# The first transformer's P V with the values in the array: dividing P on GpSimd, and whole units as pieces of the order

## The chip, the cores and the metric

The kernel runs on one core of a Trainium2 chip. A core has TensorE (PE; PEld is its weight loading), VectorE (DVE), ScalarE (ACT), GpSimd (POOL) and the queues that issue transfers (SP's is the one that matters here). The time is that of one launch in microseconds of the device; a table gives the median of three runs. The profile is of one further execution.

## The reference

x is 4 x 512 tokens of 128 features in f32. Four layers each compute `x = x + s * silu(f)`, where s and f are two sub-networks of the normalised x:

- layer 0: local and latent attention; a feed-forward with weights and inputs rounded to FP4
- layer 1: causal attention of 16 heads; a ternary gated feed-forward
- layer 2: differential attention; **a transformer of 6 layers with 16 heads of 64, local attention with a window of 32** ("the first transformer", names with `l2`)
- layer 3: a linear recurrence; a transformer of 2 layers with 8 heads and a window of 64 ("the second transformer", `l3`)

One transformer layer:

```
q, k, v = shift_tokens(x) @ Wqkv, in heads of 64
q, k = rotary(l2norm(q) * q_scale), rotary(l2norm(k) * k_scale)
sim = 8 * q k^T        # a block of W queries sees its own and the previous block of W keys
o = softmax(sim) @ v
x = x + o @ Wo
h = layernorm(shift_tokens(x)) ; a, g = h @ W1 + b1
x = x + (a * gelu(g)) @ W2 + b2
```

## The kernel before

Features lie on the partitions and tokens in the free dimension throughout: x is a tile of 128 x 2048. Everything is f32 but the masks.

`transformer` makes three generators over all rows (a row is a layer and one of the four batch elements): `queries_keys`, `attention` and `feed_forward`. The first transformer has two groups of eight heads (GP = 2), so 24 rows x 2 = 48 slots. In slot i it merges a part of each: queries and keys of slot i, attention of an earlier slot, feed-forward of an older one. Each generator yields the estimated TensorE time of the piece that it has just written, and `merge` always continues the one that has done the smallest share of its total (10.3, 20.4, and 7.7 or 1.7). So the pieces set the order of the program; the framework then places the instructions of each engine, mostly in that order, ahead of it where an instruction is ready earlier, and each engine works through its own list in order.

The attention of a slot is two units (j = 0 and 1), of four heads each, at 512 queries. Steps of a unit, with the line numbers of the profile (matrix products all show line 122 or 1389, the helper `net.mm` and the scores' own call; transposes show 126):

- `scores` (L1370): two mask matmuls, then 64 small matmuls of 64 x 32 stationary and 64 columns (L1389) on eight tiles of the array, two row halves by four column quarters; then the row maximum (L1399), two subtractions (L1403), the exponential (ACT, L1408), the row sum (L1410) and the reciprocal r (L1412)
- `turn` (L1415): eight 128x128 transposes of P, and the ACT copy into PT (L1424). It is called for the previous unit, in the middle of the scores
- `weigh` (L1427): P V. 64 small matmuls with PT stationary (64 x 32) and the values streaming (64 columns); the result has queries on the partitions, and two DVE multiplications by r put it into On (L1454)
- `turn_back` (L1465): eight transposes of On, and two ACT copies into OT (L1474)
- after the second unit, the output product: four matmuls of 512 columns with Wo, added to x (L1513)
- `values` (L1331): 16 value products of 64 columns of tokens by 256, in two halves, copied to vo (L1352); four transfers on SP (L1356, L1358) make ve, the copy of vo that is shifted by one block. Values are made two units ahead

All PSUM tiles of the transformer come from one pool of four buffers of two banks (`S2`). `queries_keys` writes each projection into such a buffer; ACT squares it (L1293), POOL adds the halves (L1294), DVE multiplies by two tables (L1295, L1297), POOL adds (L1298). `unit_length` sums the squares on TensorE, takes the root on ACT (L1317, L1318), multiplies on DVE (L1321) and moves the result by eight transfers on SP (L1328). `split` is true in the first transformer alone.

## Time and profile before

| what | value |
|---|---|
| time, median of 3 runs | 3968.79 us (3940.47 to 3970.37) |
| the profiled execution's own time | 3955.01 us |
| its span, first to last instruction | 3953.3 us |
| mean granted TensorE clock | 0.942; 0.99 to 1.00 in the first transformer |
| the first transformer lies at | about 1590 to 3410 us |
| POOL, L1298 (128x1024 addition) | 224 of 2362 ns |
| POOL, L595 (128x1024 by a broadcast, layer 1) | 48 of 1893 ns |
| ACT, L1474 (copies to OT, 128x512) | 192 of 592 ns |
| DVE, L1454 (On, 128x512) | 192, 120.5 us busy, mean 668 ns |

Busy times of one engine are added up from its instructions; a matmul's record is longer than the time that it keeps the array, since matmuls overlap. The distance from start to start of neighbouring matmuls is what one costs. An f32 matmul has two records.

### The profile page before, as it was taken

Reading aid. Unit: us, or ns where it says so; the run is one execution under the profiler, and the core shown is the slowest. Engines: PE = TensorE matmul, PEld = TensorE weight load, DVE = VectorE, ACT = ScalarE, POOL = GpSimd, SP = SyncE. Lnnn points to the kernel's source line nnn. Section 1 sums busy time; section 2 is a strip of 40 time slices with the busy share of each in tenths; the row PEclk is TensorE's granted clock in tenths of the full one; section 3 lists DMA queues with packets and bytes.
Section 4 is the critical chain, followed back from the end, with each engine's and each line's share of the span. In section 5 each row is a group of like instructions: output and inputs, shape, how many; then the busy total and the mean of one; then the engine's idle time right before and its main releaser. Section 6 shows DMA issues by size and latency. Waiting matters only on the chain.

```text
span 3953.3 us, 105287 instructions
## 1 busy us (share of the span) xinstructions
PE 3577.5 (90%) x46763; PEld 1880.3 (48%) x46891; DVE 2452.6 (62%) x3429; ACT 1845.0 (47%) x2510; POOL 1157.9 (29%) x994
## 2 busy tenths in 40 slices
PE   7786999899999998889999999999999999778887
PEld 4553455444444443444444554554444445445554
DVE  6674555413353341677777787777777777457774
ACT  3343666523133324454555554555455455535555
POOL 1000444300021112533334343343443343033220
PEclk7677999999699999999999999999999999889998
DMA  1000000001000001434344434334334333413221
GB/s 38 8 26 28 1 1 1 30 0 51 2 1 3 3 1 37 106 86 115 88 96 110 98 91 109 95 91 119 93 83 117 86 80 94 130 37 83 54 56 42
DMA packets 123574, 236.12 MB, mean 60 GB/s; under 512 B 29624, under 2 KB 44128, under 8 KB 117728
## 3 DMA queue, kind: packets, MB, share of 16 engines
q1 hardware_dynamic: 114064, 209.58, 21.7%
q10 hardware_dynamic: 8624, 19.29, 1.5%
q8 instruction: 369, 6.05, 0.6%
q0 software_dynamic: 432, 0.51, 0.1%
q14 instruction: 85, 0.70, 0.1%
HBM read 50.08 MB, written 5.54 MB: 14 GB/s over the span
## 4 chain that ended last, share of the span: by engine, by line
PE 62%; DVE 13%; ACT 12%; issue 6%; DMA 3%; POOL 2%; SPq 1%; DVEq 0%; ACTq 0%; POOLq 0%
PE S L122 39%; PE S L126 5%; PE M L122 5%; PE S L1389 4%; PE o L1094 3%; ACT l_P L581 3%; PE o L614 2%; DVE l_rot L1295 2%; DVE rotp L1297 1%; DMA l_tab<-in_k_rot_l 1%; DVE l_rot L1321 1%; PE S L1008 1%; ACT sqp L1293 1%; ACT l_PT L1424 1%; SPq L1328 1%
## 5 line engine op out<-in xcount | busy, mean ns | idle before, releaser
L1298 POOL TENSOR_TENSOR l_rot<-l_rot,rotp 128x1024 f32<-128x1024 f32 x224 | 528.6, 2362 | 324.7 <-DVE rotp L1297 313.3
L1294 POOL TENSOR_TENSOR sqp<-sqp 128x512 f32<-128x512 f32 x224 | 291.5, 1301 | 956.6 <-ACT sqp L1293 952.0
L122 PE MATMUL S<-hb,l_wqk 128*128 128x512 f32 x896 | 476.8, 622 | 38.1 <-ACT l_PT L1424 10.7
L1293 ACT ACTIVATE sqp<-S 128x1024 f32<-128x1024 f32 x224 | 230.2, 1027 | 305.1 <-PE S L122 304.1
L1321 DVE SCALAR_TENSOR_TENSOR l_rot<-S,l_rot 128x1024 f32<-128x1024 f32 x224 | 264.6, 1219 | 133.8 <-ACT S L1318 110.6
L126 PE MATMUL S<-core,l_P 128*128 128x128 f32 x1856 | 266.9, 288 | 40.1 <-ACT l_P L1408 17.3
L122 PE MATMUL S<-l_KT,l_QT 32*128 32x256 f32 (+7 forms) x1536 | 264.2, 510 | 34.7 <-ACT l_P L1116 14.5
L1295 DVE TENSOR_TENSOR l_rot<-S,l_tab 128x1024 f32<-128x1024 f32 x224 | 271.2, 1211 | 24.6 <-ACT sqp L1293 24.0
L1389 PEld LDWEIGHTS S<-l_qk 64*32 64x32 f32 (+1 forms) x13312 | 178.5, 108 | 217.7 <-issue 211.2
L1116 ACT ACTIVATE l_P<-S 128x1024 f32<-128x1024 f32 x160 | 156.7, 1022 | 252.3 <-PE S L122 251.7
L126 PEld LDWEIGHTS S<-core,l_P 128*128 128x128 f32 x1856 | 213.3, 146 | 128.1 <-issue 39.3
L1297 DVE TENSOR_TENSOR rotp<-S,l_tab 128x1024 f32<-128x1024 f32 x224 | 270.8, 1209 | 1.4 <-POOL l_rot L1298 1.3
L1389 PE MATMUL S<-l_qk 64*32 64x64 f32 (+1 forms) x13312 | 249.5, 230 | 18.8 <-DMA l_qk<-l_rot 1.7
L122 PE MATMUL S<-sqp,l_k 128*128 128x512 f32 x448 | 251.9, 648 | 13.4 <-POOL sqp L1294 6.6
L122 PE MATMUL S<-l_wv,hb 128*64 128x256 f32 (+1 forms) x1600 | 237.2, 400 | 5.5 <-DVE rotp L1297 4.2
L1069 DVE TENSOR_REDUCE l_mx<-S 128x2 f32<-128x768 f32 (+1 forms) x192 | 155.0, 864 | 136.7 <-PE S L1008 136.7
L122 PEld LDWEIGHTS S<-l_ve,l_PT 64*32 64x32 f32 (+1 forms) x6656 | 164.3, 108 | 152.5 <-issue 124.9
L1399 DVE TENSOR_REDUCE mx<-S 128x16 f32<-128x1024 f32 (+1 forms) x128 | 156.3, 1221 | 116.1 <-PE S L1389 112.2
L122 PEld LDWEIGHTS S<-hb,l_wqk 128*128 128x128 f32 x896 | 147.2, 191 | 168.6 <-issue 92.0
L122 PE MATMUL S<-l_OT,l_wo 128*128 128x512 f32 (+1 forms) x512 | 218.9, 543 | 8.3 <-DVE ffu L1551 7.9
L1120 POOL TENSOR_SCALAR_AFFINE_SELECT l_P<-l_P 128x256 f32<-128x256 f32 x256 | 99.4, 406 | 417.0 <-ACT l_P L1116 411.6
L1317 ACT ACTIVATE S<-S,l_tiny 128x1024 f32<-128x1024 f32 x112 | 121.9, 1089 | 198.4 <-PE S L122 180.2
(358 smaller groups left out, 6580.1 us busy)
## 6 DMA issues: line engine op xcount, KB each, us to landing
l_qk<-l_rot SPq DMA_DIRECT2D x896, 128.0 KB
l_ve<-l_vo SPq DMA_DIRECT2D x112, 256.0 KB
l_ve<-l_vo SPq DMA_DIRECT2D x96, 224.0 KB
l_tab<-in_k_rot_l ACTq DMA_DIRECT2D x16, 1024.0 KB
l_wqk<-in_l2Wqkv SPq DMA_DIRECT2D x12, 512.0 KB
l_wv<-in_l2Wqkv SPq DMA_DIRECT2D x12, 256.0 KB
l_wo<-in_l2Wo SPq DMA_DIRECT2D x12, 256.0 KB
l_ve<-l_vo SPq DMA_DIRECT2D x24, 128.0 KB
```

The source lines that it names most:

```text
L122: self.nc.tensor.matmul(out, lhsT, rhs, start=start, stop=stop)
L126: self.nc.tensor.transpose(out, in_, self.ident[:n, :n])
L1069: nc.vector.tensor_reduce(mxv[:, bs, 2 * m + e, 3 - i], s[u][:, :, c : c + n], axis=AX.X, op=ALU.max)
L1116: nc.scalar.activation(P[u], s[u], AF.Exp, scale=scale)
L1293: nc.scalar.activation(sq, p, AF.Square)
L1294: nc.gpsimd.tensor_tensor(sq[:, 0, :], sq[:, 0, :], sq[:, 1, :], ALU.add)
L1295: nc.vector.tensor_tensor(t[:, g], p, tab[:, 0], ALU.mult)
L1297: nc.vector.tensor_tensor(m, p, tab[:, 1], ALU.mult)
L1298: nc.gpsimd.tensor_tensor(t[:, g], t[:, g], m[:, ::-1, :], ALU.add)
L1321: nc.vector.scalar_tensor_tensor(t[:, g], p[:, g, :].unsqueeze(1).to_broadcast([128, 2, S]), 1e12, t[:, g], ALU.min, ALU.mult)
L1389: net.nc.tensor.matmul(sv[W * bl : W * bl + W, e, t, g, :].rearrange("p (s k) -> p s k", s=2), qk[0][r, g, j, W * c : W * c + W], kw, star ...
L1399: nc.vector.tensor_reduce(mx, flat, axis=AX.X, op=ALU.max)
```

## The change

In the first transformer (`split`):

- P is multiplied by r on GpSimd right after the softmax; the multiplication of On on DVE is gone
- `turn` of the previous unit is called after the softmax of the current one, not in the middle of its scores
- `weigh_turned` takes the place of `weigh` and `turn_back`: the values (64 x 64) are stationary on the four quadrants of the array and 32 columns of PT stream. The result has the head dimension on the partitions and is copied to OT directly. Blocks of odd number have the two heads' halves exchanged, so OT has a second index for the block's parity, and Wo is loaded a second time with its halves exchanged; the output product becomes 2 x 4 matmuls of 256 columns
- the values of a unit pair are made one unit ahead: the first half in the unit before, the second half in the first unit, each ahead of P V
- pieces: the scores of a unit and its P V are one piece each, marked `Small`; after a `Small` piece `merge` continues another generator. Query/key products, sums of squares and value products are handed over in pairs or halves. The attention's total is 18.6
- Wo has two buffers for three

The second transformer keeps `weigh` and `turn_back`; its output product yields after every two matmuls instead of each.

```diff
+class Small(float):
+    pass
...
 def merge(run):
     run, totals = [g for g, _ in run], [t for _, t in run]
     done = [0.0] * len(run)
+    i = piece = None
     while run:
-        i = min(range(len(run)), key=lambda k: done[k])
+        others = [k for k in range(len(run)) if k != i] if isinstance(piece, Small) else []
+        i = min(others or range(len(run)), key=lambda k: done[k])
         try:
-            done[i] += next(run[i]) / totals[i]
+            piece = next(run[i])
+            done[i] += piece / totals[i]
         except StopIteration:
+            piece = None
             del run[i], done[i], totals[i]
...
-        self.attention_weight = 20.4 if self.split else 25.0
+        self.attention_weight = 18.6 if self.split else 25.0
...
-                t = self.WT.tile([128, 4, 128], F32, name=pre + "_wo", bufs=3)
-                nc.sync.dma_start(t, a[pre + "Wo"][l][512 * gp : 512 * (gp + 1)].rearrange("(t p) n -> p t n", p=128))
+                t = self.WT.tile([128, 2 if self.split else 1, 4, 128], F32, name=pre + "_wo", bufs=2)
+                wo = a[pre + "Wo"][l][512 * gp : 512 * (gp + 1)].rearrange("(t p) n -> p t n", p=128)
+                nc.sync.dma_start(t[:, 0], wo)
+                if self.split:
+                    nc.sync.dma_start(t[0:64, 1], wo[64:128])
+                    nc.sync.dma_start(t[64:128, 1], wo[0:64])
...
                             c = 128 * (4 * g + 2 * i + h)
                             o = p[:, h, :]
                             net.mm(o.rearrange("p (s u k) -> p s u k", s=2, k=W) if i else o, w[:, c : c + 128], hk if i else hb)
-                            yield 0.86
+                            if h or not self.split:
+                                yield 1.72 if self.split else 0.86
...
         for g in range(2):
             net.mm(p[:, g, :], self.ones, sums[g][:, 0, :])
-            yield 0.86
+            if g or not self.split:
+                yield 1.72 if self.split else 0.86
...
                 if self.split:
                     for e in range(2):
                         net.mm(pv[64 * e : 64 * e + 64, k - u0, :], hb[:, 64 * k : 64 * k + 64], w[:, 256 * e : 256 * e + 256])
-                    yield 0.45
                 else:
                     c = 128 * (n * tp + k)
                     net.mm(pv[:, k - u0, :], hb[:, c : c + 128], w)
                     yield 0.86
+            if self.split:
+                yield 1.8
...
         for t in range(T):
-            if last and t == T // 2:
+            if last and t == T // 2 and not self.split:
                 yield from self.turn(last)
...
-                yield 0.31
+                if not self.split:
+                    yield 0.31
+        if self.split:
+            yield Small(2.48)
...
         nc.vector.tensor_reduce(rs, P.rearrange("p t g e k -> p (t g e) k"), axis=AX.X, op=ALU.add)
         r = net.stat(n, "r")
         nc.vector.reciprocal(r, rs)
+        if self.split:
+            Pn = P.rearrange("p t g e k -> p (t g e) k")
+            nc.gpsimd.tensor_tensor(Pn, Pn, r.unsqueeze(2).to_broadcast([128, n, 2 * W]), ALU.mult)
+            if last:
+                yield from self.turn(last)
         return P, r
...
+    def weigh_turned(self, u, OT):
+        net, W, T = self.net, self.W, self.T
+        PT, vo, ve, tp, j = (u[k] for k in ("PT", "vo", "ve", "tp", "j"))
+        o = self.S2()
+        ov = o.rearrange("p s (i x q) -> p s i x q", x=2, q=W)
+        for i in range(2 * T):
+            for bl in range(self.NB):
+                c = self.NB * (T * tp + i // 2) + bl
+                v, k = (vo if c % 2 else ve), c // 2 - tp * self.NU
+                for e in range(2):
+                    rows, d, s = slice(64 * e, 64 * e + 64), 64 * (2 * (i % 2) + j), bl % 2
+                    x = 64 * (e ^ s)
+                    net.mm(ov[x : x + 64, s, i, bl // 2, :], v[rows, k, d : d + 64], PT[rows, i, W * bl : W * bl + W])
+        yield Small(2.4)
+        for s in range(2):
+            dst = OT[:, s].rearrange("p (g j) (t q) -> p j g t q", j=2, q=2 * W)
+            self.nc.scalar.copy(dst[:, j], o[:, s, :].rearrange("p (t g q) -> p g t q", g=2, q=2 * W))
...
     def weigh(self, u):
         net, nc, W, T = self.net, self.nc, self.W, self.T
         PT, r, vo, ve, tp, j = (u[k] for k in ("PT", "r", "vo", "ve", "tp", "j"))
         On = self.PP.tile([128, 2 * T, 2, 64], F32, name=self.pre + "_On", bufs=1)
-        o = self.S2() if self.split else self.M()
+        o = self.M()
...
-                    if self.split:
-                        rows, d = slice(64 * e, 64 * e + 64), 64 * (2 * g + j)
-                        net.mm(
-                            o[W * bl : W * bl + W, e, 64 * i : 64 * i + 64], PT[rows, i, W * bl : W * bl + W],
...
-            nc.vector.tensor_tensor(
-                On.rearrange("p n e d -> p (n e) d"), o.rearrange("p (n d) -> p n d", d=64),
-                r.unsqueeze(2).to_broadcast([128, 4 * T, 64]), ALU.mult,
-            )
+                    n, d = 2 * i + e, 64 * (4 * g + 2 * j + e)
+                    net.mm(o[W * bl : W * bl + W, 64 * n : 64 * n + 64], PT[:, n, W * bl : W * bl + W], v[:, k, d : d + 64])
+            yield 0.15
+        nc.vector.tensor_tensor(
+            On.rearrange("p n e d -> p (n e) d"), o.rearrange("p (n d) -> p n d", d=64),
+            r.unsqueeze(2).to_broadcast([128, 4 * T, 64]), ALU.mult,
+        )
         u["On"] = On
...
     def turn_back(self, u, OT):
         net, T = self.net, self.T
-        t = (self.S2() if self.split else self.M().unsqueeze(1)).rearrange("p a (b q) -> p (a b) q", q=128)
+        t = self.M().rearrange("p (b q) -> p b q", q=128)
...
             if older:
-                if older["j"] == 0:
-                    OT = self.TP.tile([128, 4, 128 * T], F32, name=self.pre + "_OT", bufs=1)
-                self.turn_back(older, OT)
-                yield 0.9 if self.split else 0.45
+                if not self.split:
+                    if older["j"] == 0:
+                        OT = self.TP.tile([128, 1, 4, 128 * T], F32, name=self.pre + "_OT", bufs=1)
+                    self.turn_back(older, OT[:, 0])
+                    yield 0.45
                 if older["j"] == 1:
                     wo = self.part("o", older["l"], older["gp"])
                     p = self.M()[:, 0 : 128 * T]
-                    for t in range(4):
-                        net.mm(p, wo[:, t, :], OT[:, t, :], t == 0, t == 3)
-                        yield 0.86 if self.split else 0.43
+                    parities = 2 if self.split else 1
+                    pv = p.rearrange("p (x s q) -> p s x q", s=parities, q=W)
+                    for s in range(parities):
+                        for t in range(4):
+                            net.mm(pv[:, s], wo[:, s, t, :], OT[:, s, t, :].rearrange("p (x q) -> p x q", q=W), t == 0, t == 3)
+                            if t % 2:
+                                yield 0.86
                     ys = net.tok(self.y, older["b"])[:, 128 * T * older["tp"] : 128 * T * (older["tp"] + 1)]
                     nc.vector.tensor_tensor(ys, ys, p, ALU.add)
                 older.clear()
-            if last:
+            if last and not self.split:
                 yield from self.weigh(last)
-            if u and i + 2 < len(units) and u["j"] == 0:
+            if u and self.split:
+                if u["j"] == 0 and i:
+                    yield from until_none(ahead)
+                elif u["j"] == 1 and i + 1 < len(units):
+                    ahead = self.values(units[i + 1])
+                    yield from until_none(ahead)
+            elif u and i + 2 < len(units) and u["j"] == 0:
                 ahead = self.values(units[i + 2])
                 yield from until_none(ahead)
             elif u and i + 1 < len(units):
                 yield from until_none(ahead)
+            if last and self.split:
+                if last["j"] == 0:
+                    OT = self.TP.tile([128, 2, 4, 256], F32, name=self.pre + "_OT", bufs=1)
+                yield from self.weigh_turned(last, OT)
```

## The prediction, made before the change was run

> **What bounds the kernel now.** I read the page's busy rows, then stretches of the first transformer, then its waits, and then TensorE's timeline inside one slot, because a share of busy time does not say what a matmul costs.
>
> ```profile
> PE 3577.5 (90%) x46763; PEld 1880.3 (48%) x46891; DVE 2452.6 (62%) x3429; ACT 1845.0 (47%) x2510; POOL 1157.9 (29%) x994
> ```
>
> Busy time in a stretch of the first transformer, columns PE, weight loads, DVE, ACT, POOL, granted clock:
>
> ```profile
> 2400.00:2600.00 200.00, 191.88 (x3341) 99.11 (x3351) 156.26 (x176) 101.50 (x117) 77.24 (x46) 0.99 0.43 106
> ```
>
> TensorE works 96% of this stretch at full clock, the others 78, 51 and 39%. Between 1800 and 3200 us there are 74 units (the 74 row maxima of L1399), two to a slot: a slot lasts 1400/37 = 37.8 us, and there are 48. TensorE waits about 1.5 us per slot; its longest waits there are short and scattered:
>
> ```profile
> PE S L122 <- DVE l_On L1454: 16.1, 14, 1.4
> PE S L122 <- ACT l_PT L1424: 10.1, 25, 0.8
> ```
>
> So the set of instructions on TensorE decides, and what lies between them. The timeline (start, length, tile, shape, records; an f32 matmul is two records):
>
> ```profile
> 2412.38 0.41 PE L1389 MATMUL S<-l_qk 64*32 64x64 f32 x18
> 2412.72 1.12 PE L122 MATMUL S<-hb,l_k 128*128 128x512 f32 x2
> 2413.77 0.71 PE L1389 MATMUL S<-l_qk 64*32 64x64 f32 x46
> 2414.41 1.09 PE L126 MATMUL S<-core,l_P 128*128 128x128 f32 x8
> 2415.34 1.02 PE L122 MATMUL S<-hb,l_wqk 128*128 128x512 f32 x2
> 2416.29 0.86 PE L1389 MATMUL S<-l_qk 64*32 64x64 f32 x64
> 2417.08 1.09 PE L126 MATMUL S<-core,l_On 128*128 128x128 f32 x8
> 2418.01 1.02 PE L122 MATMUL S<-ffg,core 128*128 128x512 f32 x2
> ...
> 2421.16 1.02 PE L122 MATMUL S<-hb,l_wqk 128*128 128x512 f32 x2
> 2422.02 1.88 PE L122 MATMUL S<-l_OT,l_wo 128*128 128x512 f32 x4
> ```
>
> Starts tell the price. A full matmul among its like takes 2422.02-2421.16 = 0.86 us. Ahead of small tiles it takes 2416.29-2415.34 = 0.95, between two groups of them 2413.77-2412.72 = 1.05. The groups of 18 and 46 take 0.34 and 0.64 us: 0.30 for 28 records, so 10.7 ns each, and 0.34-18x0.0107 = 0.15 us for leaving the small tiles. **One visit to small tiles costs 0.15+0.09+0.10 = 0.34 us** beyond its records. Counting the changes of tile shape along the timeline from 1800 to 3200 us gives 484 visits from the full array, 13.1 a slot, or 4.4 us of 37.8.
>
> **The change part by part**, per slot of two units.
>
> *Turning back goes.* P V now leaves the head dimension on the partitions, so the 16 transposes of l_On fall: 2418.01-2417.08 = 0.93 us per unit, **-1.86**. Its copies stay (two of 128x512 per unit, 592 ns on ACT, the same size). The division of the output goes from DVE: 4 x 0.63 us, off the path; its buffer waits (16.1 us in 37 slots, 0.4 a slot) become waits for the ACT copies that now free it.
>
> *Whole units as pieces.* I followed the pieces through merge with their new weights. A slot's order is: a query/key pair, all scores, feed-forward, turn, a pair, eight output matmuls, a pair, values and P V at once, a pair of sums, all scores, a pair, feed-forward, turn, values and P V at once, a pair of sums. That is four visits: 9.1 fewer, at most -3.1. The trace's order departs here and there from the program's (a feed-forward pair ahead of its place), so I count eight visits: 8 x 0.34 = **-2.7**. If pieces are torn apart again: 0.
>
> *P V with V loaded.* As many records, 128 a unit, but 64 columns are loaded and 32 stream, on four quadrants instead of eight tiles. Now, and in the nearest rows where loading is longer than streaming (32 loaded, 18 streamed):
>
> ```profile
> 2406.84 0.25 PE L122 MATMUL S<-l_ve,l_PT 64*32 64x64 f32 x2
> ...
> 2407.64 0.23 PE L122 MATMUL S<-l_vo,l_PT 64*32 64x64 f32 x2
> 2407.81 0.65 PE L122 MATMUL S<-l_wv,hb 128*64 128x256 f32 x4
> ```
>
> ```profile
> 88.46 0.20 PE L122 MATMUL M<-l_ve,l_PT 128*32 128x18 f32 x1
> ...
> 88.74 0.20 PE L122 MATMUL M<-l_vo,l_PT 128*32 128x18 f32 x1
> ```
>
> The first are 80 records in 0.97-0.15 us: 10.3 ns. The second are 34 in 0.28 us: 8.5 ns, on four column tiles of one row group. Mean load times (128 columns 190 ns, 64 columns 137) give 0.83 ns a column, 27 ns for 32: a tile there comes round in 34 ns, its load and 7 more. The Trainium skill (TensorE: Matmul & The Clock Gate, Part 3, the mechanism) says that a load overlaps running matmuls only in another row group. By that, two quadrants of a row group take turns: (53+27)/2 = 40 ns a record, 5.1 us a unit, +7.5 a slot, and the change loses. But by that rule the second row would need 27+15 = 42 ns a record, and it shows 8.5. I take the row: (53+8)/4 = 15.3 ns, 1.96 us a unit against 1.35, **+1.2**. Bounds: 13.3 (loads alone) +0.7; 30 (two loads at a time) +4.9.
>
> A second rule speaks against it: the Trainium skill (TensorEngine Tiling (Array Packing), Restrictions and Gotchas, Gotcha 1) says that row tiles cannot use one PSUM bank at once, and each bank here takes both row halves, on different partitions. The second transformer's recurrence already writes four row groups into one bank:
>
> ```profile
> 3451.83 7.25 PE L741 MATMUL T<-l_x,l_LW 32*32 32x64 f32 x256 [7.30 <-DVE l_x L855]
> ```
>
> That is 28 ns a record with the clock at 0.73; one at a time would need over 64x0.83 = 53. So they run together.
>
> *Output matmuls* become 16 records of 256 columns in place of eight of 512 per slot: the same columns. The second transformer has that form, 8 records in 3601.81-3599.99 = 1.82 us less the 0.09 of leaving: 0.216 each, half of 0.43. Zero. *Weights of them*: three transfers for one, twelve times, and two buffers for three; SP now waits there 42.0 us in six waits, unseen by TensorE. A buffer still comes free a slot before it is needed; behind it on SP are query/key transfers for a later slot. Zero to 2 us each; I take zero.
>
> *P divided on GpSimd.* Nearest row: L595, the same form (128x1024 times a broadcast), 1893 ns. POOL goes from 14.6 to 18.4 us of a slot. TensorE never waits for POOL in 1800-3200 us. Its cover is a unit's length, some 17 us, before the turn. But POOL works in order: behind a division that waits for the softmax (maximum 1.22, two subtractions 1.3, exponential 1.06, sum 1.22, reciprocal 0.24) stand the additions of squares, for which the sums on TensorE wait.
>
> *Turn moved* behind the next unit's softmax, with its ACT copy (1.02). In a slot's second half only 16 value records (1.7 us) lie between the turn and its P V. If the copy stands behind that unit's exponential, counting from the end of the scores: DVE 2.4 (unit lengths), 1.2, 1.3; ACT 1.06, then the copy, 7.0; TensorE is there at 1.8+0.93+1.7 = 4.4. That wait is 2.6 us where no feed-forward piece lies between, nothing if the copy goes first. *Values* are made a unit before use instead of two to three: their four transfers (issue 0.56 and 0.70 us) stand between two sets of query/key transfers on SP and have about 15 us; landings in the chain took 2.1 us (query/key) to 6.4 (a table of 1 MB). Zero.
>
> For all new waits I put **+0.8**, less the 0.4 of the old buffer waits: +0.4. Bounds -0.4 and +5.
>
> Sum: -1.86-2.7+1.2+0.4 = **-2.96 us a slot, x48 = -142 us**.
>
> **The rivals.**
> - *POOL and ACT stand in line (slower).* The division holds the additions of squares: reciprocal at 7.4 after the scores, division 9.3, addition 10.6, while TensorE asks for the second sum at 4.4+1.96+0.86 = 7.2: 3.4 us once a slot. The late rotation behind it holds a PSUM buffer of four, and the next pair waits about its own 1.7. Then 5.1+0.3 stands for my 0.4: +2 a slot, +96, **about 4060**. It decides above 3.4 us of new waits a slot. For it: in-order queues, DVE at 78%. Against: the DVE rows show rotations slipped in ahead of a row sum that waits, so the order follows readiness.
> - *Half of it goes into waits:* -1.5 a slot, **about 3895**.
> - *It does not do what it says:* order torn up, or loads two at a time. Without the visits: -0.26 a slot, **about 3950**; with loads at 30 ns: +0.7, near 4000.
>
> **How the numbers follow.** The profiled execution took 3955.01 us, span 3953.3. Less 142: 3813. The median of the three runs is 14 above it; I say **3825**, between the two bases. Forecast 0.57 (own range 3770 to 3880), half 0.14, no effect 0.10, slower 0.19. The measurement of this kernel tells about 1% from no change (40 us). Faster 0.71, same 0.10, slower 0.19. Range: low end 9.1 visits, P V at 13.3 and no new waits, -4.3+0.2, some 3770; high end 3960, above which the slower cases lie.
>
> **What would show it.** No l_On rows; P V as 64*64 tiles with 32 columns at 14 to 17 ns from start to start; scores in groups of 128; about 35 us between every second row maximum; DVE near 27 us a slot, POOL near 18. Wrong if P V needs over 29 ns a record, if visits stay above ten, or if TensorE's waits for POOL's squares or ACT's l_PT pass 3 us a slot. The rest, outside 1590 to 3410 us, should not move.

## The result, and the profile after

The changed kernel took **4005.24 us** (median of 4, 3996.53 to 4013.39) against 3966.34 us before on the same chip: 1.0104 times as long, 95% interval 1.0078 to 1.013. It is slower by 39 us; the forecast was 3825.

Engine totals of the changed kernel:

```profile
PE 3483.6 (87%) x46379; PEld 1964.7 (49%) x46507; DVE 2353.1 (59%) x3237; ACT 1903.3 (48%) x2554; POOL 1338.5 (34%) x1090
```

TensorE is busy 94 us less and the kernel is slower all the same, so TensorE waits more. Two stretches of the first transformer (columns as before: PE, weight loads, DVE, ACT, POOL, granted clock):

```profile
2400.00:2600.00 200.00, 171.16 (x3123) 103.51 (x3134) 142.40 (x148) 102.03 (x115) 94.86 (x56) 0.96 0.41 103
2600.00:2800.00 200.00, 164.68 (x3028) 98.74 (x3032) 134.81 (x142) 104.15 (x116) 90.57 (x56) 0.96 0.39 99
```

Where 191.88 of 200 us were busy, 165 to 171 are. TensorE's waits from 1800 to 3200 us (us in total, times, longest) say for what:

```profile
PE S L122 <- DMA l_wqk<-in_l2Wqkv: 80.7, 5, 17.2
PE S L1405 <- issue: 24.2, 29, 1.8
PE S L122 <- ACT l_PT L1448: 20.6, 19, 1.2
...
PE S L122 <- DVE l_rot L1336: 8.3, 9, 0.9
```

The first was not there before at all: five waits of up to 17 us, one at each step to the next layer, for that layer's query/key weights. Slots, taken from every second row maximum, last 35.8 us on average between these steps. The five slots at the steps last 55.6, 56.0, 55.6, 56.3 and 52.5: **97 us beyond the others**.

What SP did before at the first of these steps, and what it does now (start, length, records):

```profile
1807.95 5.14 SPq L1328 DMA_DIRECT2D l_qk<-l_rot  x8
1813.19 0.53 SPq L1229 DMA_DIRECT2D l_wqk<-in_l2Wqkv  x1
```

```profile
1843.45 2.31 SPq L1374 DMA_DIRECT2D l_ve<-l_vo  x2
1852.40 5.13 SPq L1343 DMA_DIRECT2D l_qk<-l_rot  x8
1857.58 1.08 SPq L1237 DMA_DIRECT2D l_wqk<-in_l2Wqkv  x2
```

Before, the load for the first head group went out a slot ahead, at 1813, and the one for the second group at 1854. Now both stand together behind eight query/key transfers, and these start only at 1852.40. DVE and then TensorE of the changed kernel at the same place:

```profile
1845.30 1.23 DVE L1336 SCALAR_TENSOR_TENSOR l_rot<-S,l_rot 128x1024 f32<-128x1024 f32 x1 [0.22 <-issue]
1848.38 1.22 DVE L1336 SCALAR_TENSOR_TENSOR l_rot<-S,l_rot 128x1024 f32<-128x1024 f32 x1 [1.86 <-POOL l_rot L1312]
1852.43 1.42 DVE L1261 TENSOR_SCALAR l_tab<-l_tab,l_cols 128x1024 f32<-128x1024 f32 x2 [2.83 <-DMA l_tab<-in_k_rot_l]
```

```profile
1841.06 1.98 PE L122 MATMUL S<-sqp,l_k 128*128 128x512 f32 x4
...
1861.70 2.05 PE L122 MATMUL S<-hb,l_wqk 128*128 128x512 f32 x2 [16.66 <-DMA l_wqk<-in_l2Wqkv]
```

The load is issued at 1857.58 and TensorE goes on at 1861.70, 4.1 us later: the load is not slow, its place in SP's list is late. What the eight transfers wait for last is not the rotated tile. DVE ends that at 1849.60, and they go when the new layer's table (l_tab) has landed, at 1852.34. So it is at four of the five steps; only at the fifth is DVE the last. SP's own waits, 1580 to 3450 us, list the table with nine waits in all:

```profile
SPq L1343 <- DMA l_tab<-in_k_rot_l: 65.1, 9, 10.2
```

The wait has a second price. The granted clock at this step (columns: PE busy, granted clock, DMA share, GB/s):

```profile
1845.00:1850.00 5.00, 0.04 (x4) 0.88 0.95 303
1855.00:1860.00 5.00, 0.00 (x0) 0.50 0.88 208
1860.00:1865.00 5.00, 3.30 (x4) 0.50 0.55 217
```

The clock falls to half while TensorE stands, and stays there until 1865.9, 4.2 us after it goes on: the two records at 1861.70 take 2.05 us, where two such took 1.02 before. At each of the five steps the trace has such a stretch of 14 to 20 us, which ends 3 to 6 us after TensorE goes on. By estimate (half of the time in which TensorE was busy at half clock) this costs 13 us from 1800 to 3200 us, a part of what the 97 us hold beyond the 80.7 of waiting.

The rest of TensorE's timeline is as forecast. P V and scores of one unit (rows left out between):

```profile
1951.66 1.95 PE L122 MATMUL S<-l_wv,hb 128*64 128x256 f32 x16
1953.54 0.25 PE L122 MATMUL S<-l_PT,l_ve 64*64 64x32 f32 x2
...
1955.54 1.99 PE L122 MATMUL S<-sqp,l_k 128*128 128x512 f32 x4
```

```profile
1935.76 0.69 PE L1405 MATMUL S<-l_qk 64*32 64x64 f32 x45
1937.38 1.06 PE L1405 MATMUL S<-l_qk 64*32 64x64 f32 x83 [0.93 <-issue]
```

128 P V records take 1955.54-1953.54 less 0.15 for leaving, 1.85 us, 14.5 ns each (median over all units 14.6). Scores come 128 in a go, but 0.93 us passes inside this group with nothing to wait for that the profile shows. More of that below.

By stages of the two profiled executions (span 3994.8 against 3953.3, +41.5): the stretch ahead of the first transformer +10.8; the first transformer from its first query/key matmul to its last +9.5; from there to the first one of the second transformer +13.9; the second transformer's own query/key stretch +9.3; the remainder -2.0. The first of these is chance: all these kernels have the same code there, and in the executions profiled below it ends anywhere between 1577 and 1599 us.

### The profile page after: what moved, and what is told of

It reads as the page before. It is cut to its first block, busy times and chain, and to the rows that moved or that the text cites. A ratio compares the mean times of both kernels' runs of the same rounds, so it can differ in the third digit from the quotient of the medians.

```text
span 3994.8 us, 104662 instructions
## 1 busy us (share of the span) xinstructions
PE 3483.6 (87%) x46379; PEld 1964.7 (49%) x46507; DVE 2353.1 (59%) x3237; ACT 1903.3 (48%) x2554; POOL 1338.5 (34%) x1090
## 3 DMA queue, kind: packets, MB, share of 16 engines
q8 instruction: 367, 6.01, 0.6%
## 4 chain that ended last, share of the span: by engine, by line
PE 62%; DVE 12%; ACT 11%; issue 7%; DMA 3%; POOL 3%; SPq 1%; DVEq 0%; ACTq 0%; POOLq 0%
PE S L122 42%; PE M L122 5%; PE S L126 4%; PE o L1102 3%; ACT l_P L581 3%; PE S L1405 3%; DVE l_rot L1336 2%; PE o L614 2%; POOL l_rot L1312 1%; PE S L1016 1%; DVE mx L1418 1%; DVE l_rot L1309 1%; DVE rotp L1311 1%; ACT S L1332 1%; ACT l_P L1124 1%
## 5 line engine op out<-in xcount | busy, mean ns | idle before, releaser
L122 PE MATMUL S<-hb,l_wqk 128*128 128x512 f32 x896 | 459.6, 630 | 119.5 <-DMA l_wqk<-in_l2Wqkv 80.7
L1308 POOL TENSOR_TENSOR sqp<-sqp 128x512 f32<-128x512 f32 x224 | 286.3, 1278 | 664.4 <-ACT sqp L1307 664.2
L1309 DVE TENSOR_TENSOR l_rot<-S,l_tab 128x1024 f32<-128x1024 f32 x224 | 272.7, 1217 | 112.3 <-ACT sqp L1307 111.0
L122 PE MATMUL S<-l_KT,l_QT 32*128 32x256 f32 (+7 forms) x1536 | 274.0, 530 | 33.8 <-ACT l_P L1124 14.5
L122 PEld LDWEIGHTS S<-hb,l_wqk 128*128 128x128 f32 x896 | 159.5, 195 | 259.5 <-issue 199.6
L1311 DVE TENSOR_TENSOR rotp<-S,l_tab 128x1024 f32<-128x1024 f32 x224 | 270.0, 1205 | 1.3 <-POOL l_rot L1312 1.3
L1405 PE MATMUL S<-l_qk 64*32 64x64 f32 (+1 forms) x13312 | 206.5, 231 | 52.0 <-issue 33.7
L122 PE MATMUL S<-l_wv,hb 128*64 128x256 f32 (+1 forms) x1600 | 219.5, 397 | 27.7 <-ACT l_PT L1448 26.1
L122 PE MATMUL S<-sqp,l_k 128*128 128x512 f32 x448 | 227.9, 626 | 12.3 <-POOL sqp L1308 6.0
L122 PE MATMUL S<-l_OT,l_wo 128*128 128x256 f32 x896 | 211.0, 385 | 20.2 <-DVE ffu L1595 17.9
L1405 PEld LDWEIGHTS S<-l_qk 64*32 64x32 f32 (+1 forms) x13312 | 164.9, 108 | 120.4 <-issue 115.8
L122 PEld LDWEIGHTS S<-l_PT,l_ve 64*64 64x64 f32 x6144 | 191.8, 137 | 60.3 <-issue 26.8
L122 PEld LDWEIGHTS S<-l_OT,l_wo 128*128 128x128 f32 x896 | 168.2, 191 | 77.5 <-DVE ffu L1595 36.0
L1434 POOL TENSOR_TENSOR l_P<-l_P,r 128x1024 f32<-128x1024 f32 x96 | 186.3, 1940 | 57.8 <-DVE r L1431 55.6
```

What stands on the lines that cost most here:

```text
L122: self.nc.tensor.matmul(out, lhsT, rhs, start=start, stop=stop)
L1308: nc.gpsimd.tensor_tensor(sq[:, 0, :], sq[:, 0, :], sq[:, 1, :], ALU.add)
L1309: nc.vector.tensor_tensor(t[:, g], p, tab[:, 0], ALU.mult)
L1311: nc.vector.tensor_tensor(m, p, tab[:, 1], ALU.mult)
L1405: net.nc.tensor.matmul(sv[W * bl : W * bl + W, e, t, g, :].rearrange("p (s k) -> p s k", s=2), qk[0][r, g, j, W * c : W * c + W], kw, star ...
L1434: nc.gpsimd.tensor_tensor(Pn, Pn, r.unsqueeze(2).to_broadcast([128, n, 2 * W]), ALU.mult)
```

## The experiments

**What is counted.** Besides times I use two numbers per slot, from some sixteen slots near 2200 to 2800 us. A slot is the time from one unit's row maximum to that of the unit two further on. *Stalled* is the time that TensorE loses: for each pair of neighbouring matmul records, what lies more than 150 ns above the tenth-lowest distance of pairs of this kind (inside groups of small tiles, above their mean). *Own work* is the rest. Before: 37.8 us, of it 1.9 stalled and 35.9 own work. After, the steps between layers counted in: 38.3, 5.7 and 32.7.

So TensorE's own work fell by 3.2 us a slot (forecast: 1.86 + 2.7 - 1.2 = 3.4), and its waits took it all back (forecast: +0.4).

`early`, `late`, `fine`, `dve`, `combo` and `best` have 4 to 20 runs; the other eight kernels have a single run each. The twenty of `early` lie between 3949 and 3989 us, and the kernel before took 3965 to 3975 on the chips used, so a single run alone tells differences of some 20 us or more.

### The weights earlier, and the weights late in the old kernel

`early`, on the changed kernel, in `queries_keys` ahead of the slot's last `unit_length`:

```diff
                     before = sums, t
+                if self.split and b == B - 1 and l + 1 < rows[-1][0] + 1:
+                    self.part("qk", l + 1, gp)
                 made.append((yield from self.unit_length(*before)))
```

> The changed kernel, with the next layer's query/key weights asked for as soon as the last matmul that reads their buffer has been written (at the last batch row of a layer, ahead of that slot's second set of query/key transfers), not at the start of the next layer's first slot. Theory A (the late weights): in the changed kernel SP issues these weights at 1857.58 us, behind eight query/key transfers that wait for DVE, and TensorE waits 17 us for them at each of five layer boundaries; the five boundary slots last some 19 us longer than the others, 97 in all. With the weights a slot earlier the wait of L122 for l_wqk (80.7 us in five) goes below 5 us, the boundary slots come to 36 to 40 us, and the time to 4005 - 97, about 3908 (3895 to 3930), faster than the kernel before. Theory B (the wait only shows what is late anyway): the tables of the new layer and the rotation that they hold up are as late as the weights, so TensorE waits at the same place for something else; the boundary slots stay above 50 us and the time between 3970 and 4005.

`late`, on the kernel before, in `part`:

```diff
-                nc.sync.dma_start(t, a[pre + "Wqkv"][l][:, 1024 * gp : 1024 * (gp + 1)])
+                d = nc.sync.dma_start(t, a[pre + "Wqkv"][l][:, 1024 * gp : 1024 * (gp + 1)])
+                if self.split and l:
+                    self.net.tc.keep_in_program_order(d)
```

> The kernel before, with the next layer's query/key weights of the first head group held behind the query/key transfers that SP had been given before them, the place that they have in the changed kernel. Nothing else differs. Theory A (the late weights): the same wait comes up in the old kernel, 5 boundaries of 13 to 19 us each, so 3966 + 65 to 97, about 4045. Theory B (the changed slot is what makes it late): in the old order these transfers are early enough and the weights still come in time; 3960 to 3985, no wait above 3 us for l_wqk.

Measured: `early` 3975.77 us, 1.0033 (1.0019 to 1.0047) of before. `late` 4116.05 us, 1.039 (1.0359 to 1.0421). Waits of `late`:

```profile
PE S L122 <- DMA l_wqk<-in_l2Wqkv: 127.5, 9, 16.9
```

That the place of these loads in SP's list is dear is shown: the old kernel loses 151 us, with ten waits for l_wqk of 140 us in all, and its other waits are nearly what they were (l_On 19.4 us for 16.1, l_PT 9.4 for 10.1). It is more than I expected since both head groups' loads come late there, so that the step to a layer has two waits (nine in this stretch), at 14 us each.

But `early` gave back 29 us of 97. The waits for weights are gone and the new boundary slots last 38 to 42 us; in their place the other slots went from 35.8 to 37.4 on average. Waits of `early` in the same stretch:

```profile
PE S L122 <- DVE l_rot L1338: 30.1, 19, 4.8
PE S L1407 <- issue: 22.4, 29, 2.0
...
PE S L122 <- DVE rotp L1311: 15.9, 10, 3.6
PE S L122 <- DVE l_P L1424: 9.6, 9, 3.3
```

In the changed kernel the longest wait for DVE's l_rot was 0.9 us; here it is 4.8. With the load moved, the framework had set up the lists of all engines anew, so the run is not a pure removal of a wait. Theory A holds for the cause of the 97 us and fails for what their removal is worth. The time lies in the range of B, but the step slots do not stay above 50 us, and TensorE's new waits are not for the tables.

### What is late next: one step in DVE's list

DVE, and then TensorE, in `early` (start, length; in brackets the wait and for whom):

```profile
2601.66 1.21 DVE L1311 TENSOR_TENSOR rotp<-S,l_tab 128x1024 f32<-128x1024 f32 x1
2610.58 2.36 DVE L1338 SCALAR_TENSOR_TENSOR l_rot<-S,l_rot 128x1024 f32<-128x1024 f32 x2 [7.72 <-ACT S L1335]
2612.86 1.22 DVE L1309 TENSOR_TENSOR l_rot<-S,l_tab 128x1024 f32<-128x1024 f32 x1
2613.99 1.22 DVE L1311 TENSOR_TENSOR rotp<-S,l_tab 128x1024 f32<-128x1024 f32 x1
```

```profile
2600.67 1.88 PE L122 MATMUL S<-hb,l_wqk 128*128 128x512 f32 x4
2602.48 1.95 PE L122 MATMUL S<-l_wv,hb 128*64 128x256 f32 x16
...
2606.35 1.98 PE L122 MATMUL S<-sqp,l_k 128*128 128x512 f32 x4
2613.09 1.01 PE L122 MATMUL S<-l_mask,l_identb 128*128 128x512 bf16 x2 [4.75 <-DVE l_rot L1338]
```

The query/key pair of 2600.67 is done at 2602.5 and DVE is free, but next in DVE's list stands the rescaling (L1338), which waits for the exponential of the sums. TensorE does whole pieces first, values and a unit of P V, and comes to the sums at 2606.35. Until 2610.58 DVE stands still for 7.7 us; the pair's two multiplications (L1309, L1311) stand behind it, its PSUM buffer stays taken, and TensorE waits 4.75 us for a buffer. The clock falls behind this wait as well:

```profile
2612.00:2616.00 4.00, 2.91 (x54) 0.50 0.38 85
```

From 1800 to 3200 us the trace of `early` has 14 stretches at half clock, 13 of them at waits of TensorE of 1.9 to 4.8 us; before the change there are two, of 3.4 us. The same estimate of the loss is 28 us in `early` and 3 before the change.

`defer`: `unit_length` is cut in two, and the queries' rescaling with its transfers is written behind the next pair's multiplications (the early weights stay):

```diff
                         if before:
-                            made.append((yield from self.unit_length(*before)))
-                            before = None
+                            p = yield from self.sums_of(before[0])
+                            pending, before = (p, before[1]), None
+                        elif i and g:
+                            made.append(self.to_length(*pending))
```

> The kernel with the early weights, with one step of DVE moved: the rescaling of the queries (L1338) and its eight transfers are written behind the multiplications of the next pair, not ahead of them; TensorE's and ScalarE's steps stay where they are written. Theory A (DVE's order holds PSUM): DVE stands 166 us in 1800 to 3200 us at L1338 for the exponential of the sums, up to 8.8 at once, with the next pair's multiplications behind it, so that this pair's PSUM buffer is not freed and TensorE waits (4.75 us at 2608). With the step behind them TensorE's waits on l_rot, rotp and l_P (56 us in 1800 to 3200) fall below 25, a slot of 38.0 comes to about 37, and the time to 3976 - 45, about 3930 (3910 to 3950). Theory B (TensorE waits for the sum of everything DVE does, wherever the step stands): slots within 0.4 us of 38.0, time 3960 to 3990.

Measured: 3918.5 us in one run, slot 36.6 us, stalled 3.3 (`early`: 38.0 and 4.9). The same waits now:

```profile
PE S L122 <- DVE l_rot L1347: 14.7, 20, 0.9
PE S L122 <- DVE rotp L1311: 10.2, 12, 1.1
```

The long ones are gone, and the run is 57 us shorter: theory A (54 us of it in the first transformer). By the same estimate 20 us of this are clock (8 us lost here for 28). DVE itself waits for the exponential nearly as long as in the changed kernel and in `early` (in this order):

```profile
DVE l_rot L1336 <- ACT S L1333: 157.3, 34, 8.4
DVE l_rot L1338 <- ACT S L1335: 165.6, 43, 8.8
DVE l_rot L1347 <- ACT S L1340: 149.2, 36, 8.7
```

But here TensorE's buffers no longer stand behind it. `olddefer` puts the same edit into the kernel before:

> The kernel before with only the queries' rescaling moved behind the next pair's multiplications. Theory A (what the move gives belongs to the coarse pieces): in the kernel before DVE stands only 79 us at this line in 1800 to 3200 us and TensorE waits 1.3 us a slot in all, so at most 0.4 us a slot: 3945 to 3970. Rival (the old order was held up by DVE as well): 0.8 us a slot or more, below 3930.

Measured: 3976.92 us in one run, slot 37.8. The old kernel shows no gain there. `defer2` moves the keys' rescaling as well, behind the first pair of the next slot (and has the second transformer's output pieces as before):

```diff
+                        elif pending and i == g:
+                            pending[0].append(self.to_length(*pending[1:]))
+                            pending = None
...
+                if self.split and 0 < self.GP * (B * l + b) + gp < self.GP * len(rows) - 1:
+                    p = yield from self.sums_of(before[0])
+                    pending = made, p, before[1]
+                else:
+                    made.append((yield from self.unit_length(*before)))
```

> As the run before it but with the scores in one piece, and with the keys' rescaling and transfers, too, behind the next pair, which is the first pair of the next slot. In the run with the queries' step alone moved DVE still stands 239 us at this line in 1800 to 3200 us, up to 8.7 at once. If the keys' step does the same harm as the queries' did: another 0.8 to 1.4 us a slot, slot near 35.5 us, time 3850 to 3880. Rival (the keys' step at the end of a slot has nothing behind it that TensorE needs soon): slot 36.4 to 36.8, time 3900 to 3920.

Measured: 3927.59 us in one run, slot 36.7, somewhat above its rival's 3900 to 3920: no further gain shows.

### Do the two prices add?

`deferlate` has the moved rescaling without the early weights.

> The run before it without the early weights: the changed kernel with the queries' rescaling moved and the second transformer's output pieces as before. If the late weights and DVE's order are two prices that add: five waits of 13 to 17 us come back, 65 to 97 us more than with early weights, 3975 to 4007. If the stall at a layer's start lets the other engines catch up, so that part of it is given back in the slots that follow: 20 to 50 us more, 3930 to 3960.

Measured: 3982.04 us. It has second-transformer pieces as before (worth 9 us, below), so the first transformer is best compared by itself, from its first to its last query/key matmul:

```
                          weights late     weights early
rescaling in its place       1772.8           1758.1
rescaling behind the pair    1764.1           1709.6      (`best`, below; before the change: 1763.3)
```

Either mend alone gives 9 or 15 us, both give 63. They don't add. DVE's holds are there with late weights too: the changed kernel has 21 of over 4 us from 1800 to 3200 us, the longest 8.4. But TensorE then waits 0.9 us at most for l_rot, and with early weights up to 4.8: only there does the hold reach TensorE. Why it does not with late weights is not shown. Three of the five waits for weights are left in the stretch in `deferlate`, 45.7 us.

### GpSimd's division

`dve`: P divided on DVE instead of GpSimd, on `early`.

```diff
-            nc.gpsimd.tensor_tensor(Pn, Pn, r.unsqueeze(2).to_broadcast([128, n, 2 * W]), ALU.mult)
+            nc.vector.tensor_tensor(Pn, Pn, r.unsqueeze(2).to_broadcast([128, n, 2 * W]), ALU.mult)
```

> The kernel with the early weights, with P divided on DVE in place of GpSimd. The prediction's step (the division on GpSimd is off the path): two divisions of 1.2 to 1.9 us a slot go to DVE, which then works 27 to 30 of 36 us; the time stays within 20 us of the kernel with the early weights, or is up to 60 slower because DVE is late with the rotations. Rival (the division holds GpSimd's additions of squares and makes l_PT late): the wait for l_PT (20.6 us in 1800 to 3200 us) and for squares falls away and the time is 30 to 70 us lower.

Measured: 3984.04 us, 1.0041 (1.0026 to 1.0056); the interval overlaps that of `early`. A division takes 1.63 us on DVE and 1.95 on GpSimd, and its place makes no difference that this measurement tells. The rival that I had given 0.19, POOL and ACT standing in line, did not happen. TensorE's wait for l_PT in the stretch is 17.0 us with the division on GpSimd, half a microsecond a slot, and hardly less with it on DVE (`early`, then `dve`):

```profile
PE S L122 <- ACT l_PT L1450: 17.0, 18, 1.2
PE S L122 <- ACT l_PT L1450: 15.4, 20, 1.1
```

### What whole pieces are worth

`fine`: on `early`, with the pieces small as before (matmuls of a pair and of the sums one by one, values by block, scores and P V by sixteen records):

```diff
-        if self.split:
-            yield Small(2.48)
+                yield 0.31
...
-        yield Small(2.4)
+            yield 0.3
```

> The kernel with the early weights, but with the pieces small again as in the kernel before: a pair of matmuls is two pieces, scores and P V yield after each sixteen records, values after each block. The arithmetic and the place of the weights stay. The prediction's step (a visit to small tiles costs 0.34 us, eight fewer a slot): the pieces are worth 2.7 us a slot, 48 slots, so 120 to 140 us slower than the kernel with the early weights, about 4035, and visits back near 12 a slot. Rival (small pieces let other engines catch up, so TensorE waits less): only 0 to 60 us slower, with less waiting of TensorE on ACT and DVE per slot.

`oldcoarse`: the other way round, the kernel before with whole pieces (scores in two halves, since the turn lies between) and nothing else.

```diff
-                yield 0.31
+            if self.split and t % 2:
+                yield Small(1.24)
...
-            yield 0.3 if self.split else 0.15
+        if self.split:
+            yield Small(2.4)
```

> The kernel before with nothing but the coarser pieces of the first transformer: pairs of query/key and sum matmuls, values and P V of a unit as one piece each, scores as two pieces of 64 around the turn, small pieces followed by another pass; the array and the order of steps as before. The prediction's step (a visit less is 0.34 us less): six visits fewer, about 2 us a slot, so 3966 - 96, about 3870. Rival (what the visits give is waited away): TensorE's waits of 1.3 us a slot grow to 3 or more and the time stays between 3940 and 4000.

| kernel | time, us | visits | slot | stalled | own work |
|---|---|---|---|---|---|
| before | 3966 | 13.6 | 37.8 | 1.9 | 35.9 |
| `oldcoarse` | 3968 | 8.0 | 38.1 | 3.8 | 34.3 |
| after | 4005 | 6.3 | 38.3 | 5.7 | 32.7 |
| `early` | 3976 | 6.5 | 38.0 | 4.9 | 33.1 |
| `fine` | 3980 | 10.9 | 38.1 | 2.1 | 36.0 |
| `defer` | 3918 | 6.5 | 36.6 | 3.3 | 33.3 |

(Visits per slot: passages from a 128x128 tile to any smaller one, 1800 to 3200 us, value products included; the prediction counted 13.1 for the kernel before.) In the old kernel the visits have about the price that I gave them: 5.6 fewer are 1.6 us less own work, 0.29 each. In the new arithmetic small pieces cost more, 2.9 us for 4.4 visits between `early` and `fine`; what else is in it is not shown. And it buys nothing: 1.9 us more waiting in `oldcoarse`, 2.8 more in `early` against `fine`. Both rivals hold. In `oldcoarse` the wait is another one:

```profile
PE S L122 <- ACT l_OT L1491: 50.7, 37, 1.9
```

`finedefer` asks the same with DVE's step moved:

> As the first of these runs, but with the small pieces of the kernel before. With DVE's order mended, the coarse pieces can show what they are worth. If a visit costs what the prediction says and its gain is no longer waited away: some five visits more a slot, 1.5 to 2.5 us a slot, 70 to 120 us slower than with whole pieces, 3980 to 4030. If the small pieces gain from the moved step just as well: within 30 us of it.

Measured: 3969.91 us, slot 37.9, stalled 1.9, own work 36.0. Against 3923 with whole pieces (`best`, below) that is 47 us, 1.0 a slot: less than the 70 I expected at least, but a gain of whole pieces is now there. The moved step gives the small pieces nothing: their first transformer takes 1765.5 us without it and 1766.0 with it.

### Stalls inside the scores

In the changed kernel there are 29 gaps of over 200 ns inside groups of scores from 1800 to 3200 us, 30.0 us in all, and none in the kernel before. Between one long gap inside a group of small tiles and the next lie 1277, 1278, 1278, 1279, 3578, 1277, 768, 511 ... records of matmuls and weight loads: multiples of 256 each time, to one in a hundred. The page has a queue of this size:

```profile
q8 instruction: 367, 6.01, 0.6%
```

6.01 MB in 367 packets is 16.4 kB a packet, and for TensorE's 93,800 records, those of its sequencer included, 64 bytes each: one packet brings 256 instructions. The packets' own times in the trace settle it: in all 29 gaps the last packet of this queue ends 1.3 to 1.7 us before the scores go on. (From a moment taken at random the last packet lies 3.9 us back at the median, 0.5 to 11.9 for nine in ten.) The Trainium skill (Runtime: NRT & Kernel Launch, Instruction fetch mechanics) has it that code comes in blocks of 256 instructions, and that crossing into the next costs one bump of the queue, "mostly hidden". The block agrees with the trace; hidden it is not: from a stalled block's first instruction to the first of the next passed 4.8 us (median of 29). A unit's scores with their loads are 256 instructions in 1.3 us, so they use up a block before the next is there.

`halves` splits the scores into two pieces of 64 on `early`, and puts the second transformer's output pieces back:

```diff
-        if self.split:
-            yield Small(2.48)
+            if self.split and t % 2:
+                yield Small(1.24)
...
-                            if t % 2:
-                                yield 0.86
+                            if t % 2 or not self.split:
+                                yield 0.86 if self.split else 0.43
```

> The kernel with the early weights, and two edits in two stages. In the first transformer the scores of a unit are two pieces of 64 records, not one of 128. In the second transformer the output matmuls are single pieces with three weight buffers again, as in the kernel before. Theory A (the code arrives in lines): in the changed kernel some 30 stalls of about 1 us fall inside the groups of 128 scores in 1800 to 3200 us, a multiple of 256 TensorE instructions apart; a group of 128 with its loads is 256 instructions in 1.3 us. With half of it at a time the next line has time to arrive: scores fall from 4.5 to about 3.8 us a slot, less 0.34 for each visit that comes back (at most two). Slot 37.3 to 38.2. Rival (these stalls are something else, as the granted clock or a semaphore): they stay, some 25 to 30 us in that stretch. Second transformer: its slots of 54.3 come back to 51.6 us and the transformer lasts 360 us in place of 370, if the coarser output pieces made it longer.

Measured: 3956.44 us in one run; slot 37.5; gaps inside scores 6 in place of 31, 7.0 us in place of 29.2. So long dense groups are what brings most of them on (`oldcoarse`, with groups of 64, has 10). The second transformer takes 361.6 us in place of 370.5, its slots 51.8: its longer time after the change came from the coarser output pieces or from two Wo buffers in place of three; which of the two was not tried. `combo` joins `halves` and `defer`, `combo2` `halves` and `defer2`:

> Early weights, the rescaling behind the next pair's multiplications, scores in two pieces of 64, and the second transformer's output matmuls as in the kernel before: the edits of three runs together. If they add up: the rescaling gave 57 us, the second transformer's pieces 8, the halves 0.5 us a slot at most (25): 3976 - 57 - 8 - 25, about 3886; a slot of 36.2 us. If the halves give nothing once DVE no longer holds PSUM: about 3910.

> Both moves of the rescaling, scores in two pieces of 64, early weights, and the second transformer's output pieces as before. Stalls inside the scores 5 to 10 us in 1800 to 3200 us in place of 22; visits near 6.5 a slot. If the stalls were on TensorE's path they give 0.5 us a slot less the new visits' 0.34 each: within 20 us of the run with scores in one piece.

Measured: 3963.68 us, 0.9991 (0.998 to 1.0001), and 3956.81; slots 37.6 and 37.4. Both missed what I expected (3886, or 3910; within 20 us of `defer2`): they don't add either. With the halves, waits of up to 4.8 us for l_rot and 4.9 for rotp are back, and DVE stands 200 us at the rescaling, with the step in the same place of the program as in `defer`. In these runs another cut of the pieces gave new lists, and a hold came back elsewhere.

### Both mends

`best` is `early` and `defer`, scores whole, and the second transformer's output pieces and buffers as before.

> Early weights, the queries' rescaling behind the next pair's multiplications, scores of a unit in one piece, and the second transformer's output matmuls as in the kernel before. The run with the first two edits took 3918.5 us in one look with slots of 36.6 us; the second transformer's pieces give 8 more: about 3910 (3900 to 3925), faster than the kernel before by 1.2 to 1.6%.

Measured: **3923.28 us, 0.9894 of before (0.9863 to 0.9924)**: by 1.1% faster than the kernel before, and faster than the changed one. Slot 36.7, stalled 3.5, own work 33.2. What is left of the waits:

```profile
PE S L1416 <- issue: 26.9, 31, 2.1
PE S L122 <- DVE hb L1593: 16.0, 10, 1.9
PE S L122 <- DVE l_rot L1347: 14.0, 19, 0.9
```

First comes the code. From the last query/key matmul of the first transformer to the first of the second it takes 170.0 us where the kernel before takes 150.9. In the four kernels with the old arithmetic this stretch is 151 to 157 us (157 in `oldcoarse`), in the changed ones 158 to 170, small pieces included (`fine` 158.5, `finedefer` 160.6). No new queries and keys come there to fill the longer chain of a unit; that this is the reason was only argued.

## Why the prediction was wrong, by its own steps

- **Turning back, visits, P V: right in kind, the visits too dear.** No l_On rows; 14.6 ns a P V record (said 15.3, the test was 14 to 17); 6.3 visits (said eight); scores in groups of 128; own work -3.2 us a slot (said -3.4). Added up from start to start, gaps of over 0.15 us left out (2200 to 2900 us), turning back is -2.0 a slot (said -1.86), P V +0.8 (said +1.2), and all the rest -1.8, where the visits were to give -2.7 (the half clock behind the waits for weights takes back some 0.3 of it). The row of the four-column tiles was the right one to take, and the rule on loads within a row group, which the prediction cites, would have put the slot 6 us too high (+7.5 against +1.2).
- **Output matmuls: right** in the first transformer (216 ns for 256 columns). In the second, "the rest should not move" was wrong: its pieces and buffers had been changed along, +9 us, seen in the diff and not costed.
- **The step that failed first: transfers on SP at zero.** I looked at Wo and the values' four transfers, wrote "behind it on SP are query/key transfers for a later slot", and took zero. TensorE waited 80.7 us there. The order on SP is not the old one with a few transfers moved; the framework set it anew, and the next layer's query/key weights, which the diff doesn't touch, fell from a slot ahead to behind the last query/key transfers, which wait for the new table or for DVE. The five slots are 97 us longer than the others; taking the wait away gave back 29 alone. Why the framework put them there is not settled.
- **The step that failed second: "for all new waits I put +0.8"**, +0.4 net. Outside the layers' first slots a slot took 35.8 us where the sum said 34.8: of the 1.0 missing, 0.8 are stalls for code (30.0 us in 37 slots), which I had not thought of at all. With the weights early the waits were 3.0 above the old kernel's. About half of that is DVE (l_rot, rotp and l_P: 65.5 us in 1800 to 3200 where the old kernel has 11.6), its rescaling standing in order ahead of work whose buffer TensorE needed; the half clock after such waits comes on top of what a row of waits shows. My rival "POOL and ACT stand in line" was of this kind, but I had put it to GpSimd and bounded the wait by the length of a chain after the scores. It was DVE's list, and its length came from how much TensorE did ahead of the sums.
- **"If pieces are torn apart again: 0"** was the wrong doubt. The pieces stayed whole; it is that which costs waits, in the old kernel too (`oldcoarse`). The case "near 4000" comes close to 4005 by luck: it was for loads at 30 ns a record.
- **The division on GpSimd off the path: right** (`dve`). DVE went from 156 to 142 and POOL from 77 to 95 us in 200, near the 27 and 18 a slot that I gave.
- **The end of the first transformer** (+13.9 us) was left out of a sum that multiplies one slot by 48.

## What to carry to other kernels

When a change reorders the pieces of a program, list for each queue what it issues at the rare places, such as the step to a new layer, and not only in the repeating slot: a load there that the change does not touch can lose its place, and one late load costs as much as many saved visits. Work taken from the bounding engine is kept only if the engines that free its buffers can follow in their own order: put a step that waits (a rescaling that needs a sum) behind the steps that free a buffer. Small pieces cost visits but let the other engines keep up, so count both; and look at the granted clock behind each long wait.

## What the runs showed of the hardware

- TensorE's code arrives in blocks of 256 instructions, and a dense group of small matmuls outruns it: 29 stalls of 1 us in 37 slots with 128 scores in a go (256 instructions in 1.3 us), 6 with 64, none in the old kernel. A stalled block lasted 4.8 us at the median, and the code packet had ended 1.3 to 1.7 us before work went on.
- P V with 64 columns loaded and 32 streamed on four quadrants runs at 14.6 ns a record: four records start within 20 ns and the next four 58 ns after them. Both row halves write into the same PSUM bank, on different partitions.
- The granted clock was 0.96 in the changed kernel from 2400 to 2600 us, a stretch in which TensorE waits, where the kernel before had 0.99; `best` has 0.99 there again. The low clock lies at the waits: in the changed kernel it is 0.94 to 0.97 in the five windows of 200 us with a wait for weights and 0.99 to 1.00 in the two between 1800 and 3200 us without, and it falls to 0.50 behind a wait of 4.75 us as well (`early`). It falls after TensorE has stopped and comes back after it has gone on; no run changed the waits alone.
